# Projecting a batch's four blocks ahead of attention, spreading the zero stores, and spacing background pieces farther apart

## The chip, the cores and the metric

The kernel runs on one core of one Trainium2 chip. The metric is the device time of one execution in microseconds. The core has five engines that each run their own instructions in program order: TensorE (PE, with its weight loads shown as PEld), VectorE (DVE), ScalarE (ACT), GpSimd (POOL) and SyncE (SP). DMAs are issued here from SP, ACT and POOL.

## The reference

One transformer layer over 4 batches of 2048 tokens with 256 channels, in float32:

```
mod = silu(c) @ wmod                       # six rows per batch: sa, ca, ga, sb, cb, gb
ga, gb = sign * max(|g|, 0.25)
h = layernorm(x) * (1 + ca) + sa
q, k, v = split(h @ qkv_w + qkv_b)         # 16 heads of 16; rotary on q and k
x = x + ga * (softmax(causal(q k^T / 4)) v @ out_w + out_b)
h = layernorm(x) * (1 + cb) + sb
tidx, w = route(h)                         # 16 experts in 4 groups, 2 groups, then 4 experts, weights * 2.5
x = x + gb * (sum over 4 chosen experts of w * expert(h) + shared expert(h))
```

An expert is `(silu(h w1) * (h w3)) w2` with an inner width of 192.

## The kernel before, in words

The tokens are cut into 16 blocks of 512; four blocks (0 to 3, 4 to 7 and so on) are a batch. The program has an opening, an attention part and an expert part. Inside the last two, PE, ACT, DVE and POOL work in an order written out by hand: instructions are issued exactly where the Python code stands, so each engine's queue is the program order. SP's DMAs have their own queue, also in order.

**Opening.** The constants are loaded (L152 to L188), then the whole modulation matrix `wm` (L222), from which PE computes `mod` and four rows per batch; DVE turns two of the rows into gates (`gate`, L206) and the rows go to DRAM (`rowd`, L253). Then come the attention constants (L599 to L638) and the projection of block 0, `prologue(0)` with its inner function `opening` (L679): normalise, transpose (`transposed`, L283; the eviction on ACT at L652 applies the modulation), four tiles of 128 tokens through `project` (L685, matmul L689, bias adds on DVE L697 and L698), `rotate` (L705; one product on POOL and one on DVE at L711, their sum on DVE at L719) and `split` (L722; four transposes at L726, then `high_low` makes two copies on ACT, L674 and L676, and `lower` subtracts on POOL, L749). `high` and `low` are a float32 number in two parts. After two tiles each, `store` (L753) writes them with 16 DMAs of 128 KB (L762) to `qd` and `kd`; for block 0 half of them are issued by ACT, the others by SP. The values go to `vd` (L768). Then the first two units are loaded (`load`, L846), the row maxima of the first are computed (`row_max`, L866), and SP issues 32 stores of zeros (L1045, 272 KB each) into the heads of the experts' regions.

**Attention.** A unit is four heads of one block in batch 0 (16 units of 4, 8, 12 or 16 steps) and of a pair of blocks in batch 1 and up; each batch has 160 steps. A step computes one tile of 128 keys: scores on PE (L1139 for the maxima, L1146), exponential on ACT (L1154), a causal `affine_select` on POOL for the last four tiles of a block (L1158), and, one step later, `weigh` on PE (L1087). `kt`, `qt` and `vg` have three buffers; `load(u + 2)` stands at two thirds of unit u, after the blocks that it needs have been projected.

**Background.** Other work is written as generators that yield after every few instructions (a piece). `Background.pull` runs pieces, `fill` runs them as far as a `Budget` lets it. Beside the steps of attention run: row maxima of the next unit (`maxes`), the projection of later blocks (`ahead`, `prologue(1)` to `prologue(15)`; `due` says how many pieces must be done at a step, from `need`, the blocks that a unit needs), the division and output projection (`over`, `ends`), and `send` (L372, queue `after`, up to three pieces a step), which normalises a finished block, routes its tokens and scatters them to their experts' regions with 16 indirect DMAs on POOL. An empty yield between two pieces is distance: the consumer stands that much later in the program than its producer.

**Experts.** 80 pairs of tiles of 256 tokens run through `inner_a`, `inner_b` and `give` (L1314, scatter on POOL L1358). The first 56 belong to the first 12 blocks; beside them run `send` of the last four blocks and `find_tiles` (queue `late`, drained at pair 53). Beside the other 24 runs `back` (queue `rest`): the shared expert of every block (`shared`, L1392) and the sum of a block's results (`combine`, L1438). `other(2)`, `other(1)` and `other(2)` pull five pieces a pair. At the end `rest.drain()`, then the last four blocks are collected (L1386) and combined.

Of the kernel before, what the change touches and what calls it, by code (L numbers as in the profile page):

```python
# [120 lines left out]
def adaln_attention_moe(  # L121
# [33 lines left out]
    nc.sync.dma_start(gwT, gate_w)  # L155
    gbias = const.tile([P, E], F32, name="gbias")
    nc.sync.dma_start(gbias, gate_bias.partition_broadcast(P))
    bef = const.tile([P, E, E], F32, name="bef")
    nc.sync.dma_start(bef, before.partition_broadcast(P))

    sml = const.tile([P, 2 + len(PHASES), E], F32, name="sml")
    nc.sync.dma_start(sml, small.partition_broadcast(P))
    befb = const.tile([P, E, E], BF, name="befb")
    nc.vector.tensor_copy(befb, bef)
# [14 lines left out]
    for k, ph in enumerate(phases):  # L179


        ph.xs = dram.tile([E * ph.region, ROW], F32, name=f"xs{k}")

        ph.yd = dram.tile([4 * ph.tokens + 2 * ph.pairs * TT, D], F32, name=f"yd{k}")
        ph.first = sml[:, 2 + k, :]

        ph.run = const.tile([P, E], F32, name=f"run{k}")
        nc.vector.tensor_copy(ph.run, ph.first)  # L188
        ph.name = str(k)
# [16 lines left out]
    def gate(pool, g, name):  # L206

        sign = pool.tile(list(g.shape), F32, name=f"sign{name}")
        nc.vector.tensor_scalar(sign, g, 0.0, 2.0, ALU.is_ge, ALU.mult)
        nc.vector.tensor_scalar_add(sign, sign, -1.0)  # L210
        mag = pool.tile(list(g.shape), F32, name=f"mag{name}")
        nc.vector.tensor_scalar_mul(mag, g, -1.0)
        nc.vector.tensor_max(mag, mag, g)
        nc.vector.tensor_scalar_max(mag, mag, 0.25)
        nc.vector.tensor_mul(g, sign, mag)

    with tc.tile_pool(name="modw", bufs=1) as mw, tc.tile_pool(
        name="modp", bufs=1, space=PSUM
    ) as mp:
        wm = mw.tile([P, 2, 6 * D], F32, name="wm")  # L220
        nc.sync.dma_start(wm, wmod.rearrange("(k p) n -> p k n", p=P))
        sg = mw.tile([P, 2, B], F32, name="sg")  # L222
        nc.scalar.activation(sg, cT, AF.Sigmoid)
        nc.vector.tensor_mul(sg, sg, cT)
        pm = mp.tile([P, 4, B], F32, name="pm")
        for m in range(4):
            for k in range(2):
                nc.tensor.matmul(
                    pm[:, m, :],
                    lhsT=wm[:, k, m * P : (m + 1) * P],  # L230
                    rhs=sg[:, k, :],
                    start=(k == 0),
                    stop=(k == 1),
                )
        nc.vector.tensor_copy(mod, pm)
        nc.vector.tensor_scalar_add(mod[:, 2:4, :], mod[:, 2:4, :], 1.0)
        rows = mw.tile([B, 4, D], F32, name="rows")
        for m in range(4):
            pr = mp.tile([B, D], F32, name=f"pr{m}")
            for k in range(2):  # L240
                nc.tensor.matmul(
                    pr,
                    lhsT=sg[:, k, :],
                    rhs=wm[:, k, (2 + m) * D : (3 + m) * D],
                    start=(k == 0),
                    stop=(k == 1),
                )
            nc.vector.tensor_copy(rows[:, m, :], pr)
        nc.vector.tensor_scalar_add(rows[:, 2, :], rows[:, 2, :], 1.0)
        gate(mw, rows[:, 0, :], "a")  # L250
        gate(mw, rows[:, 3, :], "b")
        rowd = dram.tile([B, 4 * D], F32, name="rowd")
        nc.sync.dma_start(rowd, rows.rearrange("b m d -> b (m d)"))  # L253
# [8 lines left out]
    def normalise(xb, pools, xn):  # L262
# [11 lines left out]
        yield 0, 0, 0  # L274
# [22 lines left out]
    def route(lg, tp):  # L297
# [20 lines left out]
        def ranks(v, k, allowed):  # L318
# [20 lines left out]
            yield 0, 0, 0  # L339
# [32 lines left out]
    def send(n, xp, tp, psum, tag):  # L372
# [13 lines left out]
        for _ in range(3):  # L386
            yield 0, 0, 0
        h = yield from normalise(xb, tp, xb)
# [6 lines left out]
        yield 0, 0, 0  # L395
# [7 lines left out]
        yield 0, 0, 0  # L403
# [11 lines left out]
        re, ch, w = yield from route(lg, tp)  # L415
# [3 lines left out]
        yield 0, 0, 0  # L419
# [165 lines left out]
    with ExitStack() as actx:  # L585
# [24 lines left out]
        wqkv = acst.tile([P, 2, 3 * D], F32, name="wqkv")  # L610
        nc.sync.dma_start(wqkv, qkv_w.rearrange("(k p) n -> p k n", p=P))
        bqkv = acst.tile([P, 3 * D], F32, name="bqkv")
        nc.sync.dma_start(bqkv, qkv_b.partition_broadcast(P))
        wo = acst.tile([P, 2, D], F32, name="wo")
        nc.sync.dma_start(wo, out_w)
        ob = acst.tile([P, D], F32, name="ob")
        nc.sync.dma_start(ob, out_b.partition_broadcast(P))
        rp = acst.tile([P, T // P, 2, 2, HD // 2], F32, name="rp")
        nc.sync.dma_start(rp, rope)
# [12 lines left out]


        va_new = acst.tile([P, NG, 4, VG], F32, name="va")
        vh = va_new[:, :, :, : 4 * (HD + 1)].rearrange("p g t (h e) -> p g t h e", e=HD + 1)
        nc.gpsimd.memset(va_new, 0.0)
        for g in range(NG):
            nc.gpsimd.memset(vh[:, g, :, :, 0:1], 1.0)  # L638

        def prologue(n):  # L640
# [38 lines left out]
            def opening(hT, high_low, store):  # L679


                full = [P, 2 * H, 2, HD // 2]
                qks, rots = {}, {}

                def project(t):  # L685
                    ps = psp.tile([P, 2, BT], F32, tag="s", name="first")
                    for to, cols in ((ps[:, 0], slice(0, 2 * D)), (ps[:, 1, :D], slice(2 * D, 3 * D))):
                        for k in range(2):
                            nc.tensor.matmul(  # L689
                                to,  # L690
                                lhsT=hT[:, k, t * P : (t + 1) * P],
                                rhs=wqkv[:, k, cols],
                                start=(k == 0),
                                stop=(k == 1),
                            )
                    qk = ep.tile([P, 2, BT], F32, tag="e", name="qk0")
                    nc.vector.tensor_add(qk[:, 0], ps[:, 0], bqkv[:, : 2 * D])  # L697
                    nc.vector.tensor_add(  # L698
                        vh[:, :, t, :, 1:],
                        ps[:, 1, :D].rearrange("p (g h e) -> p g h e", g=NG, e=HD),  # L700
                        bqkv[:, 2 * D :].rearrange("p (g h e) -> p g h e", g=NG, e=HD),
                    )
                    qks[t] = qk

                def rotate(t):  # L705
                    qk = qks.pop(t)
                    parts = qk[:, 0].rearrange("p (h e two) -> p h e two", e=HD // 2, two=2)
                    prod = []
                    for s, eng in enumerate((nc.gpsimd, nc.vector)):
                        r_ = tp.tile(full, F32, tag=f"r{s}", name=f"r{s}", bufs=1)  # L710
                        eng.tensor_tensor(  # L711
                            r_,
                            parts[:, :, :, s].unsqueeze(2).to_broadcast(full),
# [872 lines left out]
```

## Time and profile before

Three runs took 3905.32 us (median), 3895.76 and 3907.83. The profiled execution took 3907.39 us, of which the span in the profile is 3905.7.

| part | from - to (us) | length | PE busy | granted PE clock |
|---|---|---|---|---|
| constants, modulation, gates | 0 - 28 | 28 | | |
| block 0 projected, stored, loaded; first maxima | 28 - 101.4 | 73.4 | 24.5 | 0.59 |
| attention, batch 0 | 101.4 - 902.0 | 800.6 | 650.5 | 0.87 |
| attention, batch 1 | 902.0 - 1557.8 | 655.8 | 585.3 | 0.92 |
| attention, batch 2 | 1557.8 - 2231.2 | 673.4 | 593.1 | 0.90 |
| attention, batch 3 | 2231.2 - 2790.0 | 558.8 | 496.8 | 0.95 |
| experts and end | 2790.0 - 3905.7 | 1115.7 | | |

The profile lists, for groups of instructions, the time that an engine was busy and the time that it sat idle before them, with the instruction that ended the wait. An idle engine costs nothing unless the end of the program waits for it. "issue" is time in which it waited for nothing that the profile shows. The granted clock is the share of full speed that TensorE was given.

### The profile page before, as it was taken

The page shows a single profiled execution, that of the slowest core. Times are in us where ns is not written, and L with a number is a line of the kernel's source. Part 1 is how long each engine was busy: PE and PEld are TensorE (multiplying, and loading weights), DVE is VectorE, ACT ScalarE, POOL GpSimd, SP SyncE. Part 2 cuts the span into 40 slices and gives each one's busy share as a digit, 9 for nine tenths or more (in the row PEclk, how much of TensorE's full clock was granted, in tenths as well). Part 3 has the DMA queues.
Part 4 walks back from the last instruction along what each step waited for, and adds up shares of the span by engine and source line. Part 5 has one row for each costly group of instructions (what it writes and reads, how often), then busy time and mean ns, then how long its engine had stood idle before and what let it go on. Part 6 is the DMA issues. An engine that isn't in the chain of part 4 may idle for free. (4 is left out here: it accounts for less than half of the span.)

```text
span 3905.7 us, 56489 instructions
## 1 busy us (share of the span) xinstructions
PE 3298.8 (84%) x20276; PEld 1723.2 (44%) x20400; DVE 2585.4 (66%) x4650; ACT 1525.6 (39%) x2188; POOL 1522.0 (39%) x2216
## 2 busy tenths in 40 slices
PE   3677988979889889888888988899888888899994
PEld 1333433434334333333433333333477676676662
DVE  2365776767776767766676777677276576667775
ACT  0233544544455544444444544455422222222220
POOL 1321243333433353244335334210155555545554
PEclk6688988989899988988988998899999898899997
DMA  5423232331333232223323322220377666688763
GB/s 163 144 84 120 98 131 101 121 118 63 109 110 123 96 117 93 81 84 102 123 101 117 104 72 71 101 96 1 114 255 242 205 226 236 216 280 303 273 248 140
DMA packets 279212, 544.96 MB, mean 140 GB/s; under 512 B 27535, under 2 KB 151439, under 8 KB 278931
## 3 DMA queue, kind: packets, MB, share of 16 engines
q1 hardware_dynamic: 249106, 461.61, 34.8%
q0 software_dynamic: 27648, 77.63, 5.3%
q8 instruction: 161, 2.64, 0.3%
q10 hardware_dynamic: 2176, 2.10, 0.2%
q14 instruction: 121, 0.98, 0.1%
HBM read 351.42 MB, written 189.81 MB: 139 GB/s over the span
## 5 line engine op out<-in xcount | busy, mean ns | idle before, releaser
L888 DVE TENSOR_REDUCE mparts<-ps 128x2 f32<-128x1024 f32 (+3 forms) x1152 | 1180.5, 1044 | 465.1 <-PE ps L878 421.1
L1154 ACT ACTIVATE e<-st 128x1024 f32<-128x1024 f32 (+3 forms) x1280 | 1078.6, 895 | 1031.3 <-PE st L1146 954.8
L878 PE MATMUL ps<-kt,qt 64*128 64x512 f32 (+3 forms) x3328 | 616.2, 415 | 187.2 <-ACT e L1154 64.8
L1087 PE MATMUL po<-e,vg 128*32 128x512 f32 (+3 forms) x5120 | 667.8, 588 | 27.4 <-POOL e L1158 15.7
L878 PEld LDWEIGHTS ps<-kt,qt 64*128 64x128 f32 x3328 | 304.7, 204 | 778.2 <-ACT e L1154 437.9
L1158 POOL TENSOR_SCALAR_AFFINE_SELECT e<-e 128x256 f32<-128x256 f32 x512 | 204.6, 410 | 964.6 <-ACT e L1154 960.7
L1255 PE MATMUL gu<-xT,wt 128*128 128x256 f32 x1920 | 462.9, 396 | 20.4 <-issue 9.5
L1358 POOL DMA_INDIRECT yd<-yt,to x320 | 315.9, 987 | 393.0 <-ACT hb L1266 200.3
L1146 PE MATMUL st<-qt,kt 64*128 64x512 f32 (+3 forms) x2560 | 461.4, 441 | 0.0
L1255 PEld LDWEIGHTS gu<-xT,wt 128*128 128x128 f32 x1920 | 370.4, 197 | 108.6 <-issue 44.0
L1139 PE MATMUL st<-mt,pick 32*128 32x512 bf16 (+3 forms) x2560 | 302.7, 375 | 74.0 <-DVE mparts L888 46.9
L477 POOL DMA_INDIRECT xs<-row,rowx x256 | 248.4, 970 | 175.0 <-DVE row L468 120.3
L911 DVE TENSOR_REDUCE mparts<-ps 128x8 f32<-128x1024 f32 x128 | 156.7, 1224 | 202.4 <-PE ps L878 191.6
L1146 PEld LDWEIGHTS st<-qt,kt 64*128 64x128 f32 x2560 | 206.1, 199 | 139.2 <-issue 127.5
L1354 ACT ACTIVATE yt<-y,of 128x256 f32<-128x256 f32 x160 | 67.1, 470 | 400.0 <-DVE is L1334 200.6
L803 POOL TENSOR_TENSOR r<-qk,rp 128x512 f32<-128x512 f32 x120 | 154.4, 1305 | 168.4 <-DVE qk L780 164.8
L1139 PEld LDWEIGHTS <-pick 32*128 32x128 bf16 x2560 | 86.9, 92 | 297.3 <-issue 285.3
L1087 PEld LDWEIGHTS po<-e,vg 128*32 128x32 f32 x5120 | 109.2, 112 | 185.8 <-issue 126.5
L749 POOL TENSOR_TENSOR low<-whole,high 128x512 fp32r<-128x512 f32 x64 | 81.4, 1271 | 258.9 <-ACT whole L676 258.7
L1293 PE MATMUL y<-wt,ha 128*128 128x256 f32 x640 | 161.7, 391 | 21.6 <-issue 18.5
L1293 PEld LDWEIGHTS y<-wt,ha 128*128 128x128 f32 x640 | 119.3, 196 | 41.8 <-issue 24.1
L776 PE MATMUL pq<-wqkv,hT 128*128 128x512 f32 x240 | 128.3, 660 | 10.4 <-ACT whole L676 8.6
(218 smaller groups left out, 3603.2 us busy)
## 6 DMA issues: line engine op xcount, KB each, us to landing
wt<-in_w_all SPq DMA_DIRECT2D x160, 640.0 KB
kt<-kd SPq DMA_DIRECT2D x124, 512.0 KB
xt<-xs SPq DMA_DIRECT2D x160, 272.0 KB
qt<-qd SPq DMA_DIRECT2D x64, 512.0 KB
yg<-yd SPq DMA_DIRECT2D x16, 2048.0 KB
vg<-vd SPq DMA_DIRECT2D x124, 168.0 KB
xb<-in_x SPq DMA_DIRECT2D x32, 512.0 KB
qd<-high SPq DMA_DIRECT2D x128, 128.0 KB
```

Source lines behind the costliest of these rows:

```text
L477: s_ = nc.gpsimd.indirect_dma_start(out=ph.xs[:, :], out_offset=bass.IndirectOffsetOnAxis(ap=rowx[:, n, t, j : j + 1], axis=0), in_=row[:, ...
L878: nc.tensor.matmul(ps[:, half, to : to + width], lhsT=qt[rows, q, t * P : (t + 1) * P], rhs=kt[rows, q, key : key + width], start=start, s ...
L888: nc.vector.tensor_reduce(to, ps[:, :, :width], AX.X, ALU.max)
L911: nc.vector.tensor_reduce(mine[:, :, :, 0], ps.rearrange("p h (t k) -> p h t k", k=P), AX.X, ALU.max,)
L1087: nc.tensor.matmul(po[32 * j : 32 * j + 32, off:], lhsT=va[:, k_, j * (HD + 1) : j * (HD + 1) + 32], rhs=es[j // 2][:, j % 2, off:], start ...
L1139: nc.tensor.matmul(sts[q][:, h_, off:], lhsT=pick[rows, :], rhs=mt[rows, off:], start=True, stop=False,)
L1146: nc.tensor.matmul(sts[q][:, h_, off:], lhsT=kt[rows, q, k_ * P : (k_ + 1) * P], rhs=qt[rows, q, off:], start=False, stop=True,)
L1154: nc.scalar.activation(es[q][:, :, off:], sts[q][:, :, off:], AF.Exp, scale=SCALE)
L1158: nc.gpsimd.affine_select(out=es[q][:, :, off : off + P], in_=es[q][:, :, off : off + P], compare_op=ALU.is_ge, fill=0.0, base=0, pattern= ...
L1255: nc.tensor.matmul(ps[:, c_ * TT : (c_ + 1) * TT], lhsT=wt[:, c_, k * 2 * I + cols : k * 2 * I + cols + P], rhs=xT[:, k, c_ * TT : (c_ + 1 ...
L1293: nc.tensor.matmul(pss[half][:, t, :], lhsT=ha[:, at_ : at_ + P], rhs=wt[:, half, 4 * I : 4 * I + D], start=(t == 0), stop=False, skip_gro ...
L1358: s_ = nc.gpsimd.indirect_dma_start(out=ph.yd[:, :], out_offset=bass.IndirectOffsetOnAxis(ap=to[:, t : t + 1], axis=0), in_=yt[:, t, :], i ...
```

## The change

All four blocks of batch 0 are projected by a new generator `opening` before attention. It works in overlapping tiles: 16 tiles of 128 tokens run through `project`, `rotate` and `split`, with block n + 1's transposes and block n + 2's normalisation in between. Its tiles use buffers of attention (`kt` for the weights `wm` and for `high` and `low`, `vg` for the values). A block's 16 stores are issued once per block, with 256 KB each, every second one by ACT. `wm` is loaded in two parts, the gates are computed after tile 6, and constants that only routing needs are loaded after the opening. The first two units are loaded after tile 10, and the first row maxima are drawn in from tile 14 on. The zeros are no longer stored in one go: the generator `heads` stands first in `after` and stores one head of a region in three pieces, so one a step. `send` takes a parameter `apart`, the number of empty pieces between a producer and its consumer on another engine: 1 beside attention as before, 3 beside experts. `shared` gets five more empty pieces. Beside the experts six pieces are pulled per pair from `late` and nine from `rest`, instead of five.

```diff
+            run(normalise(xbs[0], tp, xbs[0]))
+            modulation()
+            turned(0)
+            run(normalise(xbs[1], tp, xbs[1]))
+            project(0)
+            project(1)
+            rotate(0)
+            project(2)
+            for i in range(4 * NQ):
+                n, t = divmod(i, 4)
+                if i + 1 < 4 * NQ:
+                    rotate(i + 1)
+                if t == 0 and n + 1 < NQ:
+                    turned(n + 1)
+                if i + 3 < 4 * NQ:
+                    project(i + 3)
+                split(i)
+                if t == 1 and n + 2 < NQ:
+                    run(normalise(xbs[n + 2], tp, xbs[n + 2]))
+                if i == 6:
+                    modulation_rows()
+                yield i
```

```diff
+        def store(n, cols, high, low, queues):
+            for c_ in range(4):
+                to = (qd, kd)[c_ // 2][n].rearrange("(h part d) t -> part h d t", part=4, d=HD)
+                to = to[:, 8 * (c_ % 2) : 8 * (c_ % 2) + 8]
+                for part in range(4):
+                    of = (high, low, *((high, low) if c_ < 2 else (low, high)))[part]
+                    queues[part % 2].dma_start(to[part][:, :, cols], of[:, c_, :].bitcast(F32))
...
+            nc.sync.dma_start(wm[:, :, : 2 * D], wms[:, :, : 2 * D])
+            fetch(0)
+            nc.sync.dma_start(wqkv, qkv_w.rearrange("(k p) n -> p k n", p=P))
+            nc.sync.dma_start(bqkv, qkv_b.partition_broadcast(P))
+            nc.sync.dma_start(rp, rope)
+            for n in range(1, NQ):
+                fetch(n)
+            nc.sync.dma_start(wm[:, :, 2 * D :], wms[:, :, 2 * D :])
...
+            def turned(n):
...
+                hTs[n] = run(
+                    transposed(xbs[n], ("hT", "hT2", "aT")[n % 3], tp, pop, "po", evict)
+                )
...
+            def split(i):
+                n, t = divmod(i, 4)
+                xr = rots.pop(i)
+                if t == 0:
+                    t_ = kvp.tile([P, 2, T], FR, tag="kt", name="hl")
+                    hls[n] = t_.rearrange("p k (c t) -> p k c t", t=BT)
...
+                nc.scalar.copy(high[:, :, cols], pt)
+                whole = tp.tile([P, 4, P], F32, tag="whole", name="whole", bufs=1)
+                nc.scalar.copy(whole, pt)
+                nc.gpsimd.tensor_tensor(
+                    low[:, :, cols], whole, high[:, :, cols].bitcast(F32), ALU.subtract
+                )
+                if t == 3:
+                    store(n, slice(0, BT), high, low, (nc.sync, nc.scalar))
```

```diff
-        ahead.add(prologue(0))
-        ahead.drain()
-        ahead.pulled = 0
-        load(0)
-        load(1)
-        maxes.add(row_max(*units[0][0]))
+        for i in opening():
+            if i == 4 * NQ - 6:
+                load(0)
+                load(1)
+                maxes.add(row_max(*units[0][0]))
+            if i >= 4 * NQ - 2:
+                maxes.pull(2)
         maxes.drain()
         after_max.drain()
+        later_constants()
...
+        def heads():
+            for ph in phases:
+                for e in range(E):
+                    yield 0, 0, 0
+                    yield 0, 0, 0
+                    yield 0, 0, 0.1
+                    nc.gpsimd.memset(zeros[:, 0:1], 0.0)
+                    nc.sync.dma_start(
+                        ph.xs[e * ph.region : e * ph.region + TT, :].rearrange(
+                            "(p t) d -> p t d", p=P
+                        ),
+                        zeros.unsqueeze(1).to_broadcast([P, TC, ROW]),
+                    )
+
+        after.add(heads())
-        for n in range(1, NQ):
-            ahead.add(prologue(n))
...
-        late.add(send(n, lp, lp, banks, "b"))
+        late.add(send(n, lp, lp, banks, "b", 3))
...
-            (late if m < split else rest).pull(n)
+            if m < split:
+                late.pull(n)
+            else:
+                rest.pull(n + 1)
...
             ha = inner_a(wts_[m], xTs[m])
-            other(2)
+            other(3)
```

`later_constants` issues the loads of `gwT`, `gbias`, `bef` and `sml` on SP and the three DVE copies that need them. `project` and `rotate` of the new `opening` are those of the old one with the tile index running over all 16 tiles and a values buffer per block; `modulation_rows` computes the four rows and the gates as before.

## The prediction

> **What bounds the kernel now.** I read the busy time by stage first. The stage borders are the last `osb` copies of each batch (L1097) and the first exponential (102.82). Columns: busy us of each engine, granted TensorE clock, DMA share, GB/s.
>
> ```profile
> core 0: us, PE busy (x) PEld busy (x) DVE busy (x) ACT busy (x) POOL busy (x), PEclk, DMA share, GB/s
> 28.00:101.40 73.40, 24.46 (x91) 14.65 (x93) 22.55 (x51) 6.53 (x11) 12.70 (x16) 0.59 0.58 191
> 101.40:902.00 800.60, 650.50 (x4145) 278.61 (x4176) 504.17 (x754) 332.53 (x433) 254.57 (x330) 0.87 0.34 112
> 902.00:1557.80 655.80, 585.28 (x3972) 248.10 (x4001) 471.55 (x713) 318.45 (x411) 258.08 (x368) 0.92 0.30 101
> 2231.20:2790.00 558.80, 496.83 (x3620) 204.91 (x3646) 370.25 (x534) 294.21 (x371) 144.89 (x247) 0.95 0.20 67
> 2850.00:3600.00 750.00, 660.39 (x3221) 519.62 (x3223) 498.76 (x1369) 187.00 (x406) 407.98 (x678) 0.93 0.70 243
> ```
>
> Every batch has 160 attention steps, yet batch 0 takes 800.6 us, batch 1 takes 655.8 and batch 3 takes 558.8. PE is busy 81%, 89% and 89% of them: PE sets the pace, and work drawn in beside the steps lengthens them. Batch 3 carries no projection, batch 1 carries four, so one projected block costs (655.8 - 558.8) / 4 = 24 us there. Batch 0 carries six to seven (three of its own, three to four of batch 1's) and has the lowest clock. The first 73 us are the opposite: no engine is busy a third of them.
>
> The timeline of the opening and of the first units shows why (start, duration, in brackets the idle time before and what ended it):
>
> ```profile
> 41.28 0.69 DVE L697 TENSOR_TENSOR qk<-first,bqkv 128x512 f32<-128x512 f32 x1 [6.83 <-PE first L689]
> 42.05 1.31 POOL L711 TENSOR_TENSOR r<-qk,rp 128x512 f32<-128x512 f32 x1 [9.02 <-DVE qk L697]
> 43.86 0.69 DVE L697 TENSOR_TENSOR qk<-first,bqkv 128x512 f32<-128x512 f32 x1 [1.56 <-PE first L689]
> ...
> 54.39 4.22 ACTq L762 DMA_DIRECT2D qd<-low  x4
> ...
> 67.24 0.59 ACT L674 CAST high<-ptq 128x512 fp32r<-128x512 f32 x1 [14.75 <-DMA vg<-vd]
> ...
> 85.59 26.67 SPq L1045 DMA_DIRECT2D xs<-zeros  x32
> ...
> 102.82 1.94 ACT L1154 ACTIVATE e<-st 128x1024 f32<-128x1024 f32 x2
> ```
>
> ```profile
> 200.97 1.22 PE L878 MATMUL ps<-kt,qt 64*128 64x512 f32 x4 [13.18 <-issue]
> ...
> 356.38 1.22 PE L878 MATMUL ps<-kt,qt 64*128 64x512 f32 x4 [12.05 <-DMA qt<-qd]
> ```
>
> To be seen: a projected tile comes every 2.58 us (41.28 to 43.86), but ACT issues eight stores itself, from 54.39 to 64.35, and copies nothing until 67.24; twice PE waits 12 to 13 us because a block just projected has to be stored and loaded again.
>
> **The change, part by part** (us; minus is a gain).
>
> *Start of the opening.* The full wait for wm (1536 KB, landed 11.9) and DVE's gate arithmetic until 23.4 leave the front: only 512 KB of wm and 512 KB of x stand first on SP. At the 391 GB/s of 8 to 12 us they take 2.7, after an issue at 1.7 and a latency of 1.6 (cT issued 0.80, used 2.43): x is there at about 6 instead of 29.5. From normalise to the first projection the old kernel needs 7.3 (29.48 to 36.76). DVE then normalises block 1 as well (5 more, 29.48 to 34.45, after x1 lands near 11), so the first bias add comes at about 17.5; the first transposes of a rotated tile come 7.5 later (41.28 to 48.82), so at 25, the fourth tile's at 37 (3.9 a tile).
>
> *A block in the opening.* Engines per tile: PE 2.58 + 0.66 (four transposes) + 0.5 (a quarter of `turned`, 2.2) = 3.7; DVE 0.69 + 0.41 + 0.68 + 0.69 + 1.0 (a quarter of normalise) = 3.5; POOL 1.31 + 1.26 + some 0.5 of fills and pow = 3.1; ACT 0.58 + 0.59 + 0.4 = 1.6. Four tiles: 15. But at each block's end ACT waits for POOL's `low` (3 after the transposes) and issues eight stores in program order. Behind them on ACT stand the evictions of the next `turned`, and behind those the second half of `turned` on PE (one `po` buffer), the next projection and the next transposes: all stop. The eight took 10.0 (54.39 to 64.35) and 9.2 (71.97 to 81.18). The new stores are twice as large, 16 x 256 KB; transfers of 272 KB went out at 26.67 / 32 = 0.83 each, so 16 take 13.3 at most. I take 11. After it come eviction 0.8, transposes 1.1, projection 2.6, transposes 0.7, and three tiles at 3.5: a block lasts 3 + 11 + 5.2 + 10.5, say 29. Block ends: 37, 66, 95, 124. Tile 12 takes the buffer that block 2's stores still read (three `kt` buffers go round): 4 more, 128. Then 3 + 11 for the last stores, 1.9 for the `mt` copy and the table load (100.80 to 102.7): first exponential at about 145 instead of 102.8, **+42**. The gates, the first row maxima and the later constants lie beside ACT's issuing; if DVE waits for `bef` behind the stores, a few us more. Bounds: PE alone, no issue stall, 25 + 16 x 3.9 + 14 = 101 (-2); every block as slow as the old one, 35 (36.8 to 71.9), 17 + 4 x 35 + 17 = 174 (+71). The value lies between, next to the old block's row, from which it differs by one wait for `high`.
>
> The granted clock is the place for a rule. In the row of 44 to 48 us PE was busy 4.00 of 4 us at clock 1.00:
>
> ```profile
> 108.00:112.00 4.00, 3.64 (x23) 1.88 (x24) 1.31 (x2) 1.51 (x2) 0.81 (x2) 0.50 1.12 350
> ```
>
> yet here, with PE 91% busy and in the 20 us on either side likewise, it stayed at 0.50. I take the first row, since projections run back to back; at half clock twelve more tiles of 3.2 (2.58 + 0.66) would cost up to 38 more, which the upper bound holds. The Trainium skill, "TensorE: Matmul & The Clock Gate", Part 1 on the clock gate, says that about 3.4 us of sustained matmuls open the clock fully; by it the opening would lose next to nothing and the sum would stay, but the row above doesn't follow it.
>
> *Batch 0.* Three prologues leave it: 3 x 24 = 72. The two waits shown and 3.85 at 173.26 go, for blocks 1 to 3 are stored long before their units: 29. What late is then? Only the ordinary waits. The zeros' 26.67 us of full DMA queues (1.12 share) leave the first units, whose 129.5 us hold PE at clock 0.66: some 9 more. Together **-110**, batch 0 = 690. Bounds: only the moved work, 729 (-72); batch 3's 559 + 3.2 prologues x 24 = 636 (-165), out of reach because first-batch units are single and as short as four steps. Batch 1's 656 with four prologues is the nearest row.
>
> *Zeros, one a step.* 32 stores of 0.83 of transfer each now stand between loads on SP. Each has a POOL memset before it that overwrites what the previous store reads, so POOL waits until that has landed; behind it on POOL stand the step's affine selects, and for those PE's `po`. A step is about 4.3 and a store some 3, so most are landed. Bounds 0 and 32 x 2 = 64 if loads stand ahead; I take **+5**, near the small end because a quiet step has the room.
>
> *Pieces beside experts.* The waits of PE (total, times, longest), 2850 to 3600 and then 3600 to 3850:
>
> ```profile
> PE pt L291 <- POOL row L392: 16.6, 7, 7.5
> ...
> PE pk L426 <- DVE chb L418: 4.6, 3, 2.0
> ```
>
> ```profile
> PE y L1293 <- DVE sha L1413: 11.2, 5, 3.5
> PE y L1304 <- DVE shb L1425: 4.8, 4, 2.2
> ```
>
> With 8.6 for `sha` and `shb` in the first stretch: 45.8 that more distance can take away; I take 60%, -27. The count must fit: a late `send` grows from 62 to 76 pieces, 4 x 76 + 9 = 313, against 53 x 6 + 4 = 322 pulled before the drain (before: 257 of 268). The back pieces grow from 132 to 212; 23 x 9 + 5 = 212 are pulled (before 118 of 132). So the 14 that were left for the end move in: the last two shared blocks, 17 of PE (two of 5.4 + 3.1), **+17** inside the loop. They leave the end:
>
> ```profile
> 3839.77 8.73 DMA hTs<-hTd
> 3848.64 7.10 PE sgu L1398 x12
> 3860.50 4.42 DVE yg L1443 x2
> ```
>
> The last combine could begin when the first `yg` lands, near 3846 rather than 3860: **-14**. Net of this part **-24**; bounds +3 (no wait goes) and -43 (all go).
>
> **Sum.** +42 - 110 + 5 - 24 = -87. The profiled execution lasted 3907.39 (span 3905.7 and 1.7 around it), so 3820.4; it lies 2.1 above the median of 3905.32, which gives **3818**.
>
> **Rivals.** (1) *The opening overlaps as meant*: ACT's issues hide behind PE, first exponential near 110. For it: SP needs only 0.6 an issue; against: 14.75 us of idle ACT at 67.24. +8 - 110 + 5 - 24: 3784. (2) *The gain is eaten in part*: opening at +71, batch 0 only -72, zeros at +20, experts -10: 3914; with the last two at my values, 3885. For it: the half clock of 84 to 128. (3) *Slower*: the opening becomes bound by stores. 4.9 MB a block go out; the old stores of 128 KB each ran at 165 to 196 GB/s, and if the larger ones do no better than that while SP's loads, x and vd share the rings and ACT stands still in the issue, a block costs its 25 to 30 of transfer plus the 15 of compute that no longer overlaps, 45, and the first exponential lies near 17 + 4 x 45 + 17 = 214 (+111). It decides from a block of 51 us on (+134, what the other parts give back with the zeros at +0); with the zeros at +40 already here: 3905.3 + 111 - 110 + 40 - 24 = 3922.
>
> **How the numbers follow.** My forecast 50%, rival 1 20%, rival 2 22% (two thirds of it near 3885, the rest within 0.3%), rival 3 8%. About 0.3% is what a measurement of this kernel can tell from no change: below 3893.6 is faster. Faster 0.85 (0.50 + 0.20 + two thirds of 0.22), same 0.07, slower 0.08. The range 3752 to 3888 takes rival 1 with some of batch 0's lower bound (3784 less 32) and rival 2's nearer part; it leaves out 0.15, the rest of rival 2 and rival 3.
>
> **What would show it.** After: the exponential's first start near 145; ACT idle of about 10 at each of the first three block ends with stores before it; no PE wait above 5 for `qt` or `ps` in units 1 to 16; batch 0 near 690; waits for `row` L392 and `sha` about halved; the end after the last expert scatter about 14 shorter. The prediction is wrong if the first exponential comes after 180, or POOL waits for `zeros` in most of the first 32 steps.

## The result and the profile after

The changed kernel took 3867.06 us (median of five runs, 3865.45 to 3878.69) against 3905.32: a ratio of 0.9912, 95% interval 0.9891 to 0.9932. It is faster by 38 us, 0.7 to 1.1%, where 87 us had been forecast. Its profiled execution took 3872.93, of which the span is 3870.9.

The stage lengths of the two profiled executions tell where the time went. Borders are the first exponential, the start of the last `osb` copy of each batch, and the first fetches of `yg` (whose first one waits for the results of the first 56 pairs, a later one for those of the last 24).

| stage | before | after | difference | forecast |
|---|---|---|---|---|
| opening, to the first exponential | 102.8 | 189.9 | +87.1 | +42 |
| batch 0 | 798.7 | 713.5 | -85.2 | -110, and +5 for the zeros |
| batches 1, 2, 3 | 1888.4 | 1867.5 | -20.9 | 0 |
| sends of the last blocks and first 56 pairs | 687.9 | 674.2 | -13.7 | -27 over both pair stages |
| last 24 pairs | 361.5 | 374.9 | +13.4 | +17 |
| end | 66.4 | 50.9 | -15.5 | -14 |

The opening loses as much as batch 0 wins: batch 0 ends at 903.4 after and at 901.5 before. In this pair of profiles the gain stands in batches 1 to 3, where none was forecast, and beside the experts.

First the stretches of the changed kernel that answer to those shown of before, with one of the opening behind them (busy us of each engine, granted clock, DMA share, GB/s):

```profile
core 0: us, PE busy (x) PEld busy (x) DVE busy (x) ACT busy (x) POOL busy (x), PEclk, DMA share, GB/s
24.00:189.90 165.90, 66.67 (x246) 38.52 (x245) 63.09 (x117) 23.71 (x40) 47.05 (x45) 0.67 0.42 137
189.90:904.00 714.10, 612.31 (x3979) 257.45 (x4008) 484.44 (x715) 314.21 (x402) 219.64 (x350) 0.86 0.34 113
904.00:1550.50 646.50, 577.75 (x3967) 247.25 (x3995) 456.26 (x689) 318.87 (x410) 234.10 (x329) 0.92 0.29 99
2213.70:2771.60 557.90, 498.06 (x3620) 205.10 (x3646) 370.45 (x534) 294.96 (x371) 145.76 (x247) 0.94 0.20 67
2831.00:3580.00 749.00, 666.96 (x3264) 523.70 (x3264) 517.00 (x1391) 189.98 (x413) 418.12 (x682) 0.94 0.71 248
56.00:60.00 4.00, 0.00 (x0) 0.00 (x0) 0.00 (x0) 0.00 (x0) 0.00 (x0) 0.50 0.52 197
```

The opening is still the place where no engine is busy half of the time: PE works 67 us of 166. In the last row nothing runs at all, and the DMA engines are half busy. What they wait for is in ACT's timeline of the changed kernel (start, duration, in brackets the idle time before and what ended it; xN are N instructions of one kind in one line, and the duration is that of all):

```profile
44.30 0.59 ACT L769 CAST hl<-ptq 128x512 fp32r<-128x512 f32 x1 [7.66 <-PE ptq L762]
...
46.92 6.07 ACTq L621 DMA_DIRECT2D qd<-hl  x4
54.88 9.34 ACTq L621 DMA_DIRECT2D kd<-hl  x4
64.27 0.78 ACT L699 ACTIVATE aT<-pt,mod 128x512 f32<-128x512 f32 x1 [18.90 <-DMA kd<-hl]
...
93.47 0.59 ACT L769 CAST hl<-ptq 128x512 fp32r<-128x512 f32 x1 [15.12 <-PE ptq L762]
...
111.31 0.78 ACT L699 ACTIVATE hT<-pt,mod 128x512 f32<-128x512 f32 x1 [16.77 <-DMA kd<-hl]
...
159.73 0.59 ACT L769 CAST hl<-ptq 128x512 fp32r<-128x512 f32 x1 [30.18 <-DMA kd<-hl]
...
187.92 0.59 ACT L1023 COPY mt<-pmx 128x512 bf16<-128x512 bf16 x1 [17.19 <-DMA qd<-hl]
...
189.94 1.94 ACT L1242 ACTIVATE e<-st 128x1024 f32<-128x1024 f32 x2
```

Four times ACT issues a block's stores (from 46.92, 96.64, 130.93 and 172.11) and copies nothing until the last of them has been issued: 17.3, 14.7, 16.9 and 15.8 us. After the third it stands still another 12 (147.8 to 159.73): tile 12 waits for the buffer that block 2's stores still read. And at 93.47 it has waited 15.12 for the transposes of a tile behind the gates.

In batch 0 PE no longer waits over 4.2 us for anything; the two waits of 12 to 13 us for a block just stored are gone. PE's busy time there is 37 us less (648.7 before, 611.7 after, from the first exponential to the border) and its idle time 48 us less.

### The profile page after: what moved, and what is told of

The parts are those of the page before. It is cut to its first block, busy times and chain, and to the rows that moved or that the text cites. A ratio compares the mean times of both kernels' runs of the same rounds, so it can differ in the third digit from the quotient of the medians.

```text
span 3870.9 us, 56433 instructions
## 1 busy us (share of the span) xinstructions
PE 3282.0 (85%) x20268; PEld 1721.3 (44%) x20392; DVE 2598.7 (67%) x4672; ACT 1527.2 (39%) x2188; POOL 1502.0 (39%) x2234
## 5 line engine op out<-in xcount | busy, mean ns | idle before, releaser
L1227 PE MATMUL st<-mt,pick 32*128 32x512 bf16 (+3 forms) x2560 | 302.3, 373 | 92.5 <-DVE mparts L965 50.8
L880 POOL TENSOR_TENSOR r<-qk,rp 128x512 f32<-128x512 f32 x96 | 124.0, 1307 | 93.7 <-DVE qk L857 93.7
L1355 DVE TENSOR_TENSOR hb<-hb,gu 64x256 f32<-64x256 f32 x160 | 65.9, 412 | 102.8 <-ACT hb L1354 60.6
L841 POOL TENSOR_TENSOR low<-whole,high 128x512 fp32r<-128x512 f32 x48 | 61.2, 1275 | 172.7 <-ACT whole L837 171.9
```

The source lines that it names most:

```text
L1227: nc.tensor.matmul(sts[q][:, h_, off:], lhsT=pick[rows, :], rhs=mt[rows, off:], start=True, stop=False,)
```

## The experiments

Theory A: the opening's +87 is stores. They run on half of the DMA engines, and ACT, which issues half of them in program order, stands still until the queues have taken them; the late gates and the buffer of tile 12 come on top. Rival B: the opening is bound elsewhere (the transfers themselves, the long chain of PE, DVE and POOL at a low clock), and batch 0 gave less than forecast for the zeros' sake. All kernels compute the whole layer. They ran in three groups of four, each group on one chip; the kernel before took 3901.50, 3821.67 and 3906.51 there, so a ratio is against before on the same chip, and stages are compared within a group (the first one beside the two profiles above, whose chip is not known).

### e1: all stores issued by SP

```diff
-                    store(n, slice(0, BT), high, low, (nc.sync, nc.scalar))
+                    store(n, slice(0, BT), high, low, (nc.sync, nc.sync))
```

> The changed kernel with the opening's 16 stores a block all issued by SP, none by ACT. In the changed kernel the first exponential starts at 189.94 (before: 102.82), and ACT is held at each block's end from its first store issue until 64.2, 111.3, 147.8 and 187.9, some 17 us each. Theory A (ACT's program order is what costs; the transfers themselves can lag behind in the three buffers): the three stalls of 17 inside the opening go, blocks come every 18 to 22 us, the first exponential comes at 125 to 140, the total falls by about 50. Theory B (the transfers at their half rate are the limit, 21 us a block whoever issues them): SP takes over the whole wait, the last block waits for its buffer, and the first exponential stays above 165, the total within 20 us of the changed kernel.

Ratio 0.9787 (0.9767 to 0.9808), 3823.97 us; first exponential at 144.8 instead of 189.9, where A had 125 to 140. SP's and ACT's timelines of this kernel:

```profile
44.12 8.90 SPq L621 DMA_DIRECT2D qd<-hl  x8
53.07 10.41 SPq L621 DMA_DIRECT2D kd<-hl  x8
...
108.86 10.59 SPq L621 DMA_DIRECT2D kd<-hl  x8
...
120.74 1.01 SPq L937 DMA_DIRECT2D vg<-vd  x1
```

```profile
124.81 0.59 ACT L769 CAST hl<-ptq 128x512 fp32r<-128x512 f32 x1 [35.31 <-DMA vg<-vd]
```

The stores take SP 19 us a block (44.12 to 63.5), longer than they took ACT, but SP has nothing to compute: 45 us less for one word. What they cost was their place in ACT's program. What is left is the transfer: tile 12 still waits for its buffer, until 124.81, and the DMA share is 0.53 from 108 to 116 us, while nothing runs. (The trace names a load of `vg` as what ended the wait; on SP it stands close behind block 2's last stores, which were issued until 119.45.)

### e2: sixteen engines for each store

```diff
+                to = to.rearrange("part h d t -> part d h t")
...
-                nc.vector.tensor_add(xr, prod[0], prod[1])
+                nc.vector.tensor_add(
+                    xr.rearrange("p (c d h) -> p c h d", c=4, d=HD),
+                    *(r_.rearrange("p (c h) d -> p c h d", c=4) for r_ in prod),
+                )
```

The columns of a rotated tile are put into another order, so that a store's rows run over 16 (`d`) outermost, not over 8 heads.

> The changed kernel with the rows of the rotated tile ordered by channel and then by head, so that the destination of each store in the opening has 16 as its outermost count instead of 8; the same rows land in the same places, and half the stores stay on ACT. While the stores run alone, the changed kernel shows a DMA share of 0.51 to 0.53 and 160 to 200 GB/s, where the 32 stores of zeros in the old kernel showed 1.12 and 350. Theory A (only half of the DMA engines serve a store whose outermost count is 8): the share rises to about 1, a block's 4.2 MB take 12 instead of 21 us, ACT is held some 10 instead of 17 us a block, the wait for the last block's buffer shrinks, and the first exponential comes at 145 to 160 instead of 190; total about 30 less. Theory B (a store costs its issuing queue a fixed time of about 2 us): nothing changes, 190 +- 5.

Ratio 0.9835 (0.9791 to 0.9879), 3840.54 us; first exponential at 160.4. Two stretches of this kernel while stores run (columns as above):

```profile
52.00:60.00 8.00, 0.75 (x4) 0.75 (x5) 0.00 (x0) 0.78 (x1) 0.00 (x0) 0.50 1.03 320
124.00:132.00 8.00, 0.00 (x0) 0.00 (x0) 0.19 (x1) 0.00 (x0) 0.00 (x0) 0.54 1.04 350
```

And ACT's timeline at the end of block 1:

```profile
89.68 4.13 ACTq L623 DMA_DIRECT2D qd<-hl  x4
93.85 5.38 ACTq L623 DMA_DIRECT2D kd<-hl  x4
```

The same bytes go at 320 to 350 GB/s instead of 197, at twice the DMA share, and ACT is held 9.6 to 11.4 us a block instead of 15 to 17. The shape of the destination had halved the rate of the stores. The Trainium skill, "DMA: Bandwidth & Descriptors", section "Why a DMA increments its semaphore by 16 and not by 1", says that a transfer is spread over the largest number up to 16 that divides the outermost count on both sides; 8 and 16 here, and the shares of 0.52 and 1.03 agree. The edit also changes the order in which the rows are visited; that the count does it and not the order rests on the share.

### e3: the gates three tiles earlier

```diff
-                if i == 6:
+                if i == 3:
                     modulation_rows()
```

> The changed kernel with the four modulation rows and the gates computed after tile 3 instead of tile 6, that is beside ACT's store issues, when DVE and PE idle. In the changed kernel PE's eight products for them and DVE's copies and 15 small gate operations stand between tiles 6 and 7, where ACT waits 15.12 for the next transposes. Theory A (this is exposed time): tiles 6 and 7 close up, the first exponential comes 8 to 12 earlier (178 to 182). Theory B (hidden by the stores that follow): within 3 of 189.94.

Ratio 0.9887 (0.9854 to 0.9919), 3854.64 us; first exponential at 182.1, 7.9 earlier. ACT's timeline of this kernel at the same tile:

```profile
85.17 0.59 ACT L769 CAST hl<-ptq 128x512 fp32r<-128x512 f32 x1 [7.66 <-PE ptq L762]
```

So about half of the 15.12 wait at 93.47 was the gates' place. The other half, 7.66, stands before block 0's fourth tile too (44.30 in the changed kernel), where no gates are: there DVE works on block 2's normalisation from 34.78 to 41.55 before it turns to the tile.

### e4: the pieces beside experts as before

```diff
-                    late.add(send(n, lp, lp, banks, "b", 3))
+                    late.add(send(n, lp, lp, banks, "b"))
...
-            if m < split:
-                late.pull(n)
-            else:
-                rest.pull(n + 1)
+            (late if m < split else rest).pull(n)
...
-            other(3)
+            other(2)
```

The five more empty pieces of `shared` go too.

> The changed kernel with the pieces beside experts as before the change: one empty piece between producer and consumer, five pieces a pair, 14 pieces left over for the end. From the two traces: until the results of block 0 are fetched the experts became 13.7 shorter (687.3 to 673.6), from there to the first fetch of the last batch 13.4 longer (361.5 to 374.9), from there to the end 15.5 shorter (66.4 to 50.9). Theory A (all three come from the pieces): +14, -13, +15, total +16 against the changed kernel, so about 3883. Theory B (the first two are the run's granted clock and only the end is the pieces'): the first two stretches stay, the end gets 15 longer; total also about +15, with other stretches.

Ratio 0.9932 (0.9908 to 0.9955), 3882.16 us. The last 24 pairs fall from 374.9 to 362.3 and the end grows from 50.9 to 66.1, as forecast with the signs turned. The first 56 pairs take 681.2 instead of 674.2, 7 more where A had 14. Net 9.6 slower by stages: the direction of the term holds, its size is not -24 by this pair of profiles. The total says something else as well: without these pieces the change is still at 0.9932 of the kernel before on the same chip, so the opening, batch 0 and the zeros together gain some 0.5 to 0.9%.

### e5 to e8: the opening put together, and two parts undone

e5 joins e1, e2 and e3 and loads the first two units two tiles later (`i == 4 * NQ - 4`, for 6); e6 is e5 with half of the stores on ACT again.

> The changed kernel with four edits: 16 as the outermost count of the opening's stores, all of them on SP, the gates after tile 3, and the first two units loaded after tile 12 instead of tile 10, so that the last block takes the buffer of block 0 instead of the one that block 2's stores still read. In the run with the stores on SP alone the fourth tiles of blocks 0, 1 and 2 were copied at 43.5, 72.3 and 88.4, and tile 12 waited until 124.8 for its buffer; the gates were worth 7.9 in their own run. Theory A (the opening was held by ACT's issuing, by half-served stores and by that buffer, and by nothing else): blocks every 17 to 20, no wait at tile 12, the first exponential at 100 to 112, total 3775 to 3795. Theory B (PE, DVE and POOL interlock so that a block takes about 30 whatever the stores do): the first exponential stays at 135 or later, total above 3810.

> The same as the run before it, but with half of the stores still on ACT. It tells what ACT's issuing costs once the stores run on all DMA engines: in the run with 16 as outermost count alone ACT was held 10.5 per block (47.9 to 58.4, 89.7 to 99.2, 118.7 to 130, 148.0 to 158.3). Theory A (ACT's program order): three stalls of 10 inside and one at the end, so 30 to 40 later than with SP alone: the first exponential at 135 to 145. Theory B (with full-rate stores the issuing hides): within 10 of the run with SP alone.

e5: ratio 0.9742 (0.9717 to 0.9767), 3724.76 us against 3821.67; first exponential at 125.7, between what A and B gave. PE's timeline of e5 names the rest:

```profile
113.26 1.33 PE L960 MATMUL ps<-kt,qt 64*128 64x128 f32 x10 [8.18 <-DMA kt<-kd]
```

The first scores wait 8.18 for `kt`: with the loads moved back it is issued at 106.65, behind block 2's last stores. The two tiles had been one step too far.

e6: ratio 0.9779 (0.9748 to 0.9809), 3740.63 us; first exponential at 148.1. Issuing from ACT costs 22.4 here, although the stores run at the full rate (DMA share 0.99 to 1.01); that lies between A's 30 to 40 and B's 10 at most. In e6 ACT is held 10 to 11 us at each of four block ends. The Trainium skill, "DMA: Bandwidth & Descriptors", section "Issuing engines are not separate DMA queues", says that issuing from several engines only saves the time on the sequencer that it takes to issue; these two runs agree that nothing else was won by it, and show that the second engine's own work paid.

> The changed kernel with only the pieces beside the last 24 pairs as before the change: five a pair, 14 left for the end; the sends beside the first 56 pairs keep three empty pieces. Theory A (the two halves of that edit cancel, because what leaves the end stands on PE inside the loop): the stretch from the first fetch of results to the first fetch of the last batch falls from 374.9 to about 362, the end grows from 50.9 to 66, total within 3 of the changed kernel. Theory B (the spacing is what gains): total 10 or more above it.

> The changed kernel with the 32 zero stores issued in one go by SP after the opening, without the small writes on POOL. Theory A (spreading them pays because 8.9 MB at about 350 GB/s, 26 us, otherwise stand ahead of the loads of the third and fourth unit): batch 0 after the first exponential grows from 713.5 by 8 to 20. Theory B (POOL's waits for each store, some 45 us in all by the trace and partly exposed, cost as much as the contention): batch 0 stays within 5, or falls.

e7 undoes the pieces beside the last 24 pairs alone (`other(3 if m < split else 2)`, the old pull, and `shared` as before): 3786.85 us, ratio 0.9909 (0.9877 to 0.9940). e8 keeps all but the zeros, which go out in one loop of 32 stores after the opening, without POOL's memsets: 3786.21 us, ratio 0.9913 (0.9881 to 0.9945). Each shows its edit where the other has none. Beside the last 24 pairs and at the end the two kinds of pieces come to the same sum: 361.9 + 66.2 = 428.1 in e7, 377.2 + 50.8 = 428.0 in e8. Batch 0 takes 692.6 with the zeros spread (e7) and 692.7 with all at once (e8); the first exponential comes at 187.0 and 191.1. So in sum the spreading costs nothing and is worth 4 us at most. These two runs show only the sum: what the steps cost and what the missing burst gains could cancel.

The changed kernel's waits speak for a small cost. Of POOL's 32 memsets these two waited longest:

```profile
270.29 0.10 POOL L1133 MEMSET zeros<- 128x1 f32 x1 [5.25 <-DMA xs<-zeros]
...
354.23 0.10 POOL L1133 MEMSET zeros<- 128x1 f32 x1 [8.96 <-DMA xs<-zeros]
```

POOL waits for a store in 14 of the 32 steps, 41.6 us in all, but PE waited directly behind it once, 2.5 us.

### e9 to e12: the loads split, and the parts alone

e9 is e5 with the first unit loaded at tile 10 and the second at tile 12; e10 is the changed kernel with that split alone:

```diff
             if i == 4 * NQ - 6:
                 load(0)
-                load(1)
                 maxes.add(row_max(*units[0][0]))
+            if i == 4 * NQ - 4:
+                load(1)
```

> As the run with all four edits, but the first unit is loaded after tile 10 again and only the second after tile 12, so that the last block takes the buffer of block 1. In the run with all four edits the first exponential came at 125.7; the loads then stood behind block 2's stores on SP, PE's first score products waited 8.18 for kt, tile 15's transposes stood behind them in PE's order (10.3 of idle ACT), and the last stores ended that much later. Theory A (those 10 and what follows are the loads' place): no wait for kt, the first exponential at 108 to 116. Theory B (the last tiles are held by the stores that still run): 122 or later.

> The changed kernel with only the load of the second unit moved from tile 10 to tile 12. In the changed kernel tile 12's high copy came at 159.73, 12 after ACT's last issue of block 2 (147.8), because the last block takes the buffer that block 2's stores read. Theory A (the buffer costs its 12): tile 12 follows ACT's last issue within 3, the first exponential comes 8 to 14 earlier than 187 to 191. Theory B (the queue is full anyway, so the last block's stores end at the same time): less than 4.

e9: ratio 0.9747 (0.9722 to 0.9772), 3807.88 us against 3906.51; first exponential at 117.45, where A gave 108 to 116, and no wait for `kt`. The busiest stretch for DVE in the opening then (columns as above):

```profile
92.00:100.00 8.00, 2.91 (x13) 1.71 (x11) 7.89 (x8) 1.64 (x4) 4.93 (x4) 0.74 0.81 244
```

DVE is busy 7.89 of 8 us, beside POOL. From 36 to 116 us it is busy 61 of 80, PE 50; that DVE bounds this opening was not tried.

e10: ratio 0.9909 (0.9876 to 0.9942). ACT's timeline of e10:

```profile
139.61 8.74 ACTq L621 DMA_DIRECT2D kd<-hl  x4
148.54 0.58 ACT L769 CAST hl<-ptq 128x512 fp32r<-128x512 f32 x1 [18.01 <-DMA kd<-hl]
...
169.76 10.62 ACTq L621 DMA_DIRECT2D kd<-hl  x4
```

Tile 12 follows ACT's last issue at once (139.61 + 8.74 = 148.35, next 148.54): the buffer wait of 12 us is gone. The three buffers go round in the order of the code, so with the second unit's load behind tile 12 the last block takes the buffer of block 1, stored long before, instead of block 2's. But the first exponential comes only 7.5 earlier, at 182.44, where A had 8 to 14 and B less than 4: the last block's issues now hold ACT 19.5 (160.86 to 180.38) instead of 15.8, which fits a load of `kt` that SP now issues at 160.55, just before them (SP's own order is not that of the code: the first unit's `qt` goes out at 60.03, ahead of block 1's stores at 94.47). In the total, 3866.56 us, nothing of it is to be seen beside the change's own 0.9912.

e11 is the kernel before with only the pieces beside experts changed, e12 the kernel before itself in the same group, for its profile (3903.22 us).

> The kernel before with only the pieces beside experts changed (three empty pieces in send, five more in shared, six and nine pulled a pair). The prediction gave this part -24: -27 of waits, +17 of work moved in, -14 at the end. Theory A (the runs so far: the sends gain 7 to 14, the rest cancels to within 2): ratio 0.996 to 0.9985. Theory B (the prediction's -24): ratio 0.994 or less. Theory C (no gain beyond the moved work): 0.999 to 1.001.

> The kernel before, unchanged, for its stages on the same chip as the runs beside it; the stretch of the first 56 pairs took 675 to 690 on one chip and 620 on another, so stages are compared within a chip alone. Every theory expects the first exponential at 102 to 104, batch 0 at 790 to 800 less what a faster chip takes off, and the end at 66.

| stage | e12 (before) | e11 (pieces alone) | difference |
|---|---|---|---|
| sends and first 56 pairs | 692.9 | 670.2 | -22.7 |
| last 24 pairs | 359.8 | 377.2 | +17.4 |
| end | 66.3 | 51.4 | -14.9 |

Together -20.2, where -24 was forecast; e11's ratio is 0.9964 (0.9947 to 0.9980), 3889.65 us. The stages give 20 and the total 17. Batch 0 is the same in both, 805.5 and 805.8; e9 and e10 have 718.0 and 704.2 there, 87 and 101 less on the same chip. The 14 between these two go with the granted clock, 0.86 and 0.89, and with PE's busy time, 614.1 and 597.1, for the same number of matmuls. Batches 1 to 3 together take 1874.2 in e12 and 1869.9, 1874.9 and 1878.0 in e9, e10 and e11: on this chip the change takes nothing from them, so the 21 us of the first table can't be put down to it. In the first table's two profiles 17 of the 21 us are busy time of PE (1675.7 and 1659.0) for nearly the same count of matmuls (11584 and 11579), and batch 2's clock is 0.90 and 0.92.

## Why the prediction was wrong in size

**The direction** came out, but not in the way that was worked out. Batch 0 was to win 105 with the zeros and the opening to lose 42; in the first pair of profiles they come to -85.2 and +87.1, which leaves nothing. On the chip of e9 to e12 the change with one load moved (e10) comes to -101.4 and +79.8 against e12, a gain of 22, some 7.5 of it by e10's own edit. That the change without the pieces gains 0.5 to 0.9% (e4) is measured; in which stage it gains is not settled. The forecast was 49 us too low. Against the profiled execution it missed 52 (3872.9 - 3820.4): +45 in the opening, +20 in batch 0 with the zeros and +8 beside the experts, less the 21 of batches 1 to 3. Those 21 were not forecast and did not come again on the chip of e9 to e12: that the miss is not larger is luck.

**The step that failed** is *a block in the opening*: "so 16 take 13.3 at most. I take 11." The 0.83 us a store were read from the stores of zeros, at the full share of the DMA engines. The new stores run at 0.52, since their destination has eight outermost rows: 15 to 17 us of ACT a block. The row that would have told it was in the prediction, in rival 3: the old stores of 128 KB, with the same shape, ran at 165 to 196 GB/s. A row of before with these stores (columns as above; the zeros' row in the prediction has 1.12 and 350):

```profile
56.00:60.00 4.00, 0.14 (x1) 0.00 (x0) 0.69 (x1) 0.00 (x0) 0.79 (x1) 0.50 0.53 165
```

The size of the transfer was taken for what sets the rate; its shape did. Rival 3 priced it at 45 us a block with nothing overlapped; the first exponential at 189.9 lies between the term's own upper bound of 174 and that rival's 214, and past the 180 from which the prediction called itself wrong.

From block to block, by the starts of ACT's issues (forecast: block ends at 37, 66, 95, 128, and 3 more each): the first comes at 46.9 instead of 40 (+7; the wait before block 0's fourth tile stands in it), the second after 49.7 instead of 29 (+21: the issue 6, the gates 8 by e3; the remaining 7 were not taken apart, but the wait of 7.66 that e3 leaves is near it), the third after 34.3 instead of 29 (+5: the issue 4), the last after 41.2 instead of 33 (+8: the issue 6, tile 12's buffer 8, since it cost 12 instead of 4, and the rest 6 less than forecast), and the first exponential 17.8 later instead of 14 (+4: the issue 5). That is the 45 us between 144.8 forecast and 189.9. The mis-sized issue is 21 of them (64.7 us in the four blocks instead of 44), the gates 8 and the buffer 8, where the sum had the gates at nothing and the buffer at 4. The other 8 are parts of either sign. "If DVE waits for `bef` behind the stores, a few us more" was said of the gates and not put into the sum.

**The mechanism of the step** was right: ACT's issues stop the chain, and without them (e1) the first exponential comes at 144.8. That this is also the forecast's 145 is chance: there the stores were assumed short, here they are long and beside ACT's program.

**Batch 0**: -85 in the first pair of profiles, -87 and -101 on the chip of e9 to e12, against -105 with the zeros. The two named waits went, 25 of the 48 us of idle time that PE lost. PE's busy time fell by 37; the forecast had put the three moved projections at 72 of the stage. The clock of the stage did not rise (0.87 before, 0.86 after). A third `send` falls into batch 0 now: its last scatter lies at 829.5, inside, where before it lay at 992.3, behind the border; what that adds to the stage was not measured.

**Zeros**: the forecast had +5 for the steps and "some 9 more" won by the burst leaving the first units, -4 in sum. e7 and e8 show the sum alone: 0.1 in batch 0, 4 in the first exponential. Neither of the two terms is shown. The clock of the first units, for which the 9 stood, did not rise with the burst gone: 0.66 before, and 0.62 in the first 83 us of attention after.

**Pieces beside experts**: -20.2 instead of -24 (e11 against e12), with +17.4 and -14.9 for +17 and -14. The -27 from shorter waits is -22.7, but not where it was said. PE's waits (total, times, longest), first two of before from 2850 to 3600 us, then the changed kernel's from 2831 to 3580 and from 3580 to 3830 us:

```profile
PE y L1293 <- issue: 18.5, 17, 2.0
...
PE y L1304 <- issue: 10.6, 9, 1.8
```

```profile
PE y L1381 <- issue: 22.2, 17, 2.2
PE y L1392 <- issue: 18.4, 13, 2.2
PE pt L257 <- POOL row L365: 7.1, 4, 3.4
```

```profile
PE y L1381 <- DVE sha L1502: 11.8, 3, 4.6
PE y L1392 <- DVE shb L1515: 1.4, 4, 0.5
```

`row` fell from 16.6 to 7.1 and `shb` from 4.8 to 1.4, but `sha` rose from 11.2 to 11.8, in fewer and longer waits. The part beside the last 24 pairs moves its work and gains nothing (e7 against e8); in e11 the whole gain stands beside the first 56, where the sends are.

**The version that follows**: the change with its stores on SP, sixteen engines wide, gates after tile 3 and the loads later (e5, e9) is at 0.9742 and 0.9747 of the kernel before on two chips, against 0.9912 for the change as it was.

## What to carry to other kernels

A DMA that a computing engine issues costs that engine the whole time until the queue has taken it, here 10 to 17 us for eight stores: put stores in the program of an engine that computes nothing, and read the idle time behind each issue. Read a transfer's rate from a row of the same shape, outermost count first, not of the same size; a DMA share that stood at half while no engine worked was here the sign of a shape that used half of the DMA engines. What is moved ahead of a phase is on the path there with all its waits, so the term for the opening deserves the widest bounds.

## What the runs showed of the hardware

Some of VectorE's instructions take longer beside GpSimd. From the changed kernel's timeline, DVE's normalisation early in the opening and beside two instructions on POOL, and the durations of single ones (ns: least, median, most):

```profile
10.70 1.38 DVE L244 TENSOR_SCALAR xb<-xb,mv,rs 128x256 f32<-128x256 f32 x4 [1.16 <-POOL rs L238]
...
38.26 1.31 POOL L743 TENSOR_TENSOR r<-qk,rp 128x512 f32<-128x512 f32 x1
39.52 1.31 POOL L772 TENSOR_TENSOR hl<-whole,hl 128x512 fp32r<-128x512 f32 x1
38.33 3.30 DVE L244 TENSOR_SCALAR xb<-xb,mv,rs 128x256 f32<-128x256 f32 x4 [1.13 <-POOL rs L238]
```

```profile
L244 DVE TENSOR_SCALAR xb<-xb,mv,rs x4: 409/410/414, 10.7 to 11.7; 128x256 f32<-128x256 f32 x4
L244 DVE TENSOR_SCALAR xb<-xb,mv,rs x2: 1348/1366/1383, 38.3 to 39.6; 128x256 f32<-128x256 f32 x2
```

The four take 0.41 us each in the first place. In the second the first two, which run while POOL is at work, take 1.38 and 1.35, and the two after POOL's end at 40.83 take 0.40; that it is POOL that slows them was not tried by a run. e2's rotation add, written with a stride, takes 1.09 instead of 0.69. In e9 three of these adds in a row take 2.13, each begun within 0.1 us of a subtraction on POOL, and the next, begun without one, 1.08.

The granted clock did not follow PE's busy time alone: after the change it was 0.62 in the first 83 us of attention (190 to 273) with PE busy 71.1 us, and 0.93 in the next 83 with PE busy 69.4. Before the change it stayed at 0.50 from 108 to 132 us with PE busy 20.2 of 24. And PE's waits on "issue" in the lines of `y` shown above (29 us at their places in before, 41 after) are there in every kernel on two of the chips and in none on the third, where before takes 3821.67 and the first 56 pairs of e5 to e8 619 to 622 us instead of 664 to 693. What makes that difference between chips was not tried.
